# Silu and sigmoid of the second layer from exp and ln, in smaller steps, in a two-layer kernel on one core

## The chip, the cores and the metric

One core of one Trainium2 chip runs the kernel. The metric is the device time in microseconds: the median of three runs before is 5545.22 us (5544.22 to 5549.63).

## What is computed

The reference puts two layers on x (8 x 1024 x 256, float32). Layer 0 is a mixture of experts, causal attention and again the experts. Layer 1 is a channel mix, a selective scan and again the channel mix. The change touches layer 1 alone, of which this matters:

```python
# channel mix (before and behind the scan), on layernorm(x)
r = jax.nn.sigmoid(xr @ W_r.T)
out = r * (square(relu(xk @ W_k.T)) @ W_v.T)
# selective scan, 512 channels x 16 states
u, z = jnp.split(einsum('bld,ed->bel', h, in_proj_w), 2, axis=1)
uc = silu(causal_conv4(u) + conv_b)
delta = softplus(dt_proj(x_proj(uc)))
state = exp(delta * A) * state + delta * B * uc      # along 1024 steps
y = (sum_n state * C + uc * D) * silu(z)
```

## The kernel before

Layer 1 works by sequences (8), each in four chunks of 128 channels. 16 channels' worth of lines by 8 states lie on the 128 partitions, so that a chunk needs 16 scans along 1024 steps, a sequence 64 and the layer 512. `run` (L1597) writes the order of the scans out by hand. One turn of its loop is: `decay(i + 1)`, an exp by ACT (L1648) from a line spread by DMA into one of two PSUM tiles h; `feed(i + 2)`, a product by POOL (L1639); the scan by DVE (L1740), in place in h; the product hc with C by DVE (L1745), after which h is free. Every fourth turn PE adds the products up (L1665). Engines take their instructions in order, so this order is also the order of waiting.

All other work of the layer hangs in between as lists of steps, one Python generator each: "2before" is the channel mix of the next sequence, its normalisation, input projection and convolution (`steps_before`, with `steps_mix`); "1gate" is softplus of the next chunk and silu(z) of this one (`steps_gate`, `steps_delta`); "2low" the small projections; "3behind" what comes behind the scans. `Steps.turn` (L1578), called twice a turn, lets each list go on by its pace: a list collects due time at work / scans (L1717: 175 us in 48 scans for "2before"), each step takes its own estimate off, and at most three steps of a list go at once. What isn't through by its end is drained, all steps in a row (L1725, L1730). A step says what it needs: `hold` keeps PE and the two spare PSUM banks for its list until the next step, `gap` asks for turns of distance, `when` for a condition. For the first sequence nothing of this lies beside scans; its steps are drained before the first one (L1698, L1700).

`Pipe` (L1163) holds back the instruction that takes a full bank over until the next bank is filled. The three steps of this change go another way: both halves of a gate (L1286), of the convolution (L1391) and of z (L1442) are filled into both banks, and then one step of 3.8 us takes both over with the sigmoid (L1296) or silu (L1400, L1509), and calls `tables()` (L1154), which asks ACT for the table that holds exp and ln together:

```python
self.net.nc.scalar.preload_act_table_set("natural_log_exp_and_others")
```

`run` calls it once at its head too. Softplus (L1470 to L1484) is made of exp, ln and three POOL products in four pieces of 256 columns; its tile sp_e has one buffer.

Of the kernel before, what the change touches and what calls it, by code (L numbers as in the profile page):

```python
# [8 lines left out]
F32 = mybir.dt.float32  # L9
# [8 lines left out]
P = 128  # L18
# [20 lines left out]
DI = 512  # L39
# [1022 lines left out]
class Layer1:  # L1062
# [17 lines left out]
    def __init__(self, net, pool, Wr_t, Wk_t, Wv_t, mu_r, mu_k, ln_gamma, ln_beta, in_t, conv_w,  # L1080
                 conv_b, xp_t, dtp_t, dtp_b, A_log, Dp, out_t):
        self.net, nc = net, net.nc

        def column(name, ap, n):
            t = pool.tile([P, n], F32, name=name)
            nc.sync.dma_start(t, ap.rearrange("(c p) -> p c", p=P))
            return t

        self.mixed = {}
        for n, w, mu in (("r", Wr_t, mu_r), ("k", Wk_t, mu_k)):
            m = column(f"cm_m{n}", mu, KC)
            w0 = pool.tile([P, KC, D], F32, name=f"cm_w{n}0")
            nc.sync.dma_start(w0, w.rearrange("(k p) d -> p k d", p=P))
            w1 = pool.tile([P, KC, D], F32, name=f"cm_w{n}1")
            n1 = pool.tile([P, KC], F32, name=f"cm_n{n}")
            nc.vector.tensor_scalar(n1, m, -1.0, 1.0, ALU.mult, ALU.add)
            for k in range(KC):
                nc.vector.tensor_scalar(w1[:, k, :], w0[:, k, :], n1[:, k : k + 1], None, ALU.mult)  # L1100
                nc.vector.tensor_scalar(w0[:, k, :], w0[:, k, :], m[:, k : k + 1], None, ALU.mult)
            self.mixed[n] = (w1, w0)
        self.wv = pool.tile([P, KC, D], F32, name="cm_wv")
        nc.sync.dma_start(self.wv, Wv_t.rearrange("(k p) d -> p k d", p=P))
        self.gamma = column("ln_g", ln_gamma, KC)
        self.beta = column("ln_b", ln_beta, KC)
        self.conv_b = column("conv_b", conv_b, NDC)
        self.skip = column("skip", Dp, NDC)
        self.w_in = pool.tile([P, KC, 2 * DI], F32, name="w_in")
        nc.sync.dma_start(self.w_in, in_t.rearrange("(k p) e -> p k e", p=P))  # L1110
        self.taps = pool.tile([P, NDC, TAPS], F32, name="taps")
        nc.sync.dma_start(self.taps, conv_w.rearrange("(c p) o k -> p c (o k)", p=P))
        self.w_x = pool.tile([P, NDC, RK + 2 * NS], F32, name="w_x")
        nc.sync.dma_start(self.w_x, xp_t.rearrange("(c p) e -> p c e", p=P))


        self.XR = RK + 2 * NS
        self.w_dt = pool.tile([self.XR + 1, DI], F32, name="w_dt")
        nc.gpsimd.memset(self.w_dt[RK : self.XR, :], 0.0)
        nc.sync.dma_start(self.w_dt[0:RK, :], dtp_t)  # L1120
        nc.sync.dma_start(self.w_dt[self.XR : self.XR + 1, :], dtp_b.unsqueeze(0))
        self.w_out = pool.tile([P, NDC, D], F32, name="w_out")
        nc.sync.dma_start(self.w_out, out_t.rearrange("(c p) e -> p c e", p=P))

        n = DI // self.G
        self.A = pool.tile([P, self.PARTS, n], F32, name="A")
        with net.tc.tile_pool(name="l1_al", bufs=1) as once, net.tc.tile_pool(
            name="l1_a", bufs=1, space=PSUM
        ) as ps:
            al = once.tile([n, self.PARTS, P], F32, name="al")  # L1130
            a0 = once.tile([n, self.G, NS], F32, name="al0")
            nc.sync.dma_start(a0, A_log.rearrange("(i d) n -> i d n", d=self.G))
            pa = ps.tile([P, self.PARTS, n], F32, name="pa")
            for i in range(self.PARTS):
                nc.vector.tensor_copy(
                    al[:, i, :].rearrange("i (d n) -> i d n", n=self.NP),
                    a0[:, :, i * self.NP : (i + 1) * self.NP],
                )
                nc.tensor.transpose(pa[:, i, :], al[:, i, :], net.ident[0:n, 0:n])
            nc.scalar.activation(self.A, pa, AF.Exp)  # L1140
        nc.vector.tensor_scalar(self.A, self.A, -1.0, None, ALU.mult)

        one = pool.tile([P, self.G], F32, name="pick1")
        nc.vector.tensor_reduce(
            one, net.ident.rearrange("p (d n) -> p d n", n=self.NP), AX.X, ALU.add
        )
        self.pick = pool.tile([P, self.RG // self.G, self.RG], F32, name="pick")
        nc.gpsimd.memset(self.pick, 0.0)
        for j in range(self.RG // self.G):
            nc.gpsimd.tensor_copy(self.pick[:, j, j * self.G : (j + 1) * self.G], one)  # L1150
        self.minus = pool.tile([P, 1], F32, name="minus")
        nc.gpsimd.memset(self.minus, -1.0)
# [26 lines left out]
    def rsqrt(self, small, r, v):  # L1179
# [9 lines left out]
        nc.gpsimd.tensor_scalar(t, t, -0.5, 1.5, ALU.mult, ALU.add)  # L1189
        nc.gpsimd.tensor_tensor(r, r, t, ALU.mult)  # L1190

    def minus_mean(self, small, mv, r, name):

        off = small.tile([P, self.net.NT], F32, name=name)
        self.net.nc.gpsimd.tensor_tensor(off, mv[:, :, 0], r, ALU.mult)
        self.net.nc.gpsimd.tensor_scalar(off, off, -1.0, None, ALU.mult)
        return off
# [37 lines left out]
    def steps_mix(self, q, pools, pipe, x):  # L1235
# [20 lines left out]
        for t0 in range(0, T, W):  # L1256
# [21 lines left out]
            for i in range(0, W, 2 * P):  # L1278
# [10 lines left out]
                            )  # L1289
                got.append((i, pr))  # L1290
                pipe.filled(None)
            yield need(act=3.8, banks=True)
            gates = []
            for i, pr in got:
                r = pools["r"].tile([P, 2, D], F32, name="cm_r")
                nc.scalar.activation(r, pr, AF.Sigmoid)  # L1296
                gates.append((i, r))
            self.tables()
            for i, r in gates:
                yield need(pe=1.7, dve=0.7, pool=1.3)  # L1300
                pv = self.bank(pools, [P, 2, D], "pv")
# [15 lines left out]
    def steps_before(self, q, pools, pipe, load, keep_x):  # L1317
# [44 lines left out]
        for c in range(NDC):  # L1362
# [18 lines left out]
            tap = pools["tap"].tile([P, TAPS, P], F32, name="tap")  # L1381
            for k in range(TAPS):
                nc.scalar.mul(tap[:, k, :], net.ident, self.taps[:, c, k : k + 1])
            got = []
            for t0 in range(0, T, W):
                for k in range(TAPS):
                    if k % 2 == 0:
                        yield need(pe=1.7, hold=True, when=q.room)
                    if k == 0:
                        pc = self.bank(pools, [P, W], "pc")  # L1390
                    nc.tensor.matmul(  # L1391
                        pc, tap[:, k, :], u[:, k + t0 : k + t0 + W],
                        start=(k == 0), stop=(k == TAPS - 1),
                    )
                got.append((t0, pc))
                pipe.filled(None)
            yield need(act=3.8, banks=True, gap=1)
            o = pools["uc"].tile([P, T], F32, name="uc")
            for t0, pc in got:
                nc.scalar.activation(  # L1400
                    o[:, t0 : t0 + W], pc, AF.Silu, bias=self.conv_b[:, c : c + 1]
                )
            self.tables()
            q.uc.append(o)

    def steps_low(self, q, pools, pipe):
# [41 lines left out]
    def steps_delta(self, q, c, pools, pipe):  # L1448
# [22 lines left out]
        w = W // 2  # L1471
        for t0 in range(0, T, w):
            t = slice(t0, t0 + w)
            yield need(act=1.2, gap=1 if t0 else 0)
            e1 = pools["sp1"].tile([P, 2, w], F32, name="sp_e1")
            nc.scalar.activation(e1[:, 0, :], e[:, t], AF.Identity, bias=net.ones[:, 0:1])
            nc.scalar.activation(e1[:, 1, :], e1[:, 0, :], AF.Identity, bias=self.minus)
# [2 lines left out]
            nc.gpsimd.tensor_tensor(e1[:, 1, :], e1[:, 1, :], e[:, t], ALU.subtract)  # L1480
            nc.gpsimd.tensor_tensor(dl[:, t], dl[:, t], e1[:, 0, :], ALU.add)
            nc.gpsimd.tensor_tensor(dl[:, t], dl[:, t], e1[:, 1, :], ALU.subtract)
        yield need(pool=2.3, gap=1)
        nc.gpsimd.tensor_tensor(du, dl, q.uc[c], ALU.mult)  # L1484
        q.steps[c] = self.sent(pools, "dl", c, dl)
# [9 lines left out]
    def steps_gate(self, q, c, pools, pipe):  # L1495

        nc = self.net.nc
        T, W = self.net.T, self.W
        if c + 1 < NDC:
            yield from self.steps_delta(q, c + 1, pools, pipe)  # L1500
        got = []
        for t0 in range(0, T, W):
            yield need(pe=1.7, hold=True)
            got.append((t0, self.in_proj(q, pools, DI + c * P, t0)))
            pipe.filled(None)
        yield need(act=3.8, banks=True)
        q.zs = pools["zs"].tile([P, T], F32, name="zs")
        for t0, pz in got:
            nc.scalar.activation(q.zs[:, t0 : t0 + W], pz, AF.Silu)  # L1509
        self.tables()  # L1510

    def steps_behind(self, q, pools, pipe, load, store, when):

# [83 lines left out]
    def run(self, pools, load, load_x, keep_x, store):  # L1597
# [111 lines left out]
        for i, (b, c, l, p) in enumerate(order):  # L1709
            k = i % NS  # L1710
            if k == 2:
                if c == 0:
                    if b > 0:
                        side.drain("3behind")
                        side.add("3behind", behind(b - 1), 85, 56)
                    if b + 1 < B:
                        side.add("2before", before(b + 1), 175, 48)  # L1717
            if k == (0 if 0 < c < NDC - 1 else 2):
                side.add(
                    "1gate", self.steps_gate(seqs[b], c, pools, pipe),  # L1720
# [39 lines left out]
def kernel(  # L1760
# [102 lines left out]
    with ExitStack() as st:  # L1863
# [5 lines left out]
        with tc.manual_schedule():  # L1869
            with ExitStack() as ro:  # L1870
# [4 lines left out]
            name: pool_in(st, f"l1_{name}", bufs) for name, bufs in (  # L1875
                ("x", 2), ("mixT", 1), ("ka", 2), ("r", 2), ("hT", 2), ("u", 1), ("uc", 2 * NDC),
                ("xd", 1), ("delta", 1), ("du", 1), ("sp1", 1), ("zs", 1),
                ("rep", 1), ("sdl", 3), ("sdu", 3), ("dbu", 2), ("hc", 6), ("tap", 1), ("xn", 2), ("small", 2),
            )
        }  # L1880
        pools["dram"] = dram2
# [57 lines left out]
```

## Time and profile before

| what | us |
|---|---|
| median of three runs | 5545.22 |
| the profiled execution, its own time | 5545.59 |
| its span | 5543.9 |
| first scan starts (L1740) | 2920.8 |
| last product hc ends (L1745) | 5465.4 |
| ACT's table loads in lines of layer 1 | 194 x 1.283 |

The page gives the busy time of each engine (PE is the matrix engine, DVE, ACT and POOL the vector, activation and general engines). A row of a group has the line, the engine, the operation, the tiles as out<-in, the count, the busy time, the mean of one in ns, and behind the second bar the idle time of the engine ahead of it and who ended it. A row of the waits has who waited for whom, the sum in us, how often, and the longest. A row of the timeline has start and duration in us. In the row of a stage each engine has its busy time and count, followed by the granted clock of the matrix engine, the DMA share and GB/s.

### The profile page before, as it was taken

How to read it: one execution, taken by the hardware profiler on the slowest of the kernel's cores; microseconds unless marked ns; L12 is line 12 of the kernel's file. 1: busy time of each engine (PE TensorE's matmuls, PEld its weight loads, DVE VectorE, ACT ScalarE, POOL GpSimd, SP SyncE). 2: the span in 40 equal slices, each digit the busy share in tenths (PEclk: the TensorE clock that was granted, in tenths of full speed). 3: DMA queues.
4: the chain of work that ended last, by engine and by line, in shares of the span. 5: the costliest groups of instructions: out<-in, count | busy, mean ns of one | idle time of the engine just before them, and what ended most of it. 6: DMA issues, size and time to landing. Idle time of an engine off the chain costs nothing.

```text
span 5543.9 us, 60312 instructions
## 1 busy us (share of the span) xinstructions
PE 4501.1 (81%) x21046; PEld 2165.4 (39%) x21046; DVE 3400.8 (61%) x5590; ACT 2562.0 (46%) x4374; POOL 2388.7 (43%) x2089
## 2 busy tenths in 40 slices
PE   5699699999999998499766768788787778877767
PEld 5365434444444443265432233233333324333224
DVE  5632166666666764633107777778777777777884
ACT  2111145665566554011145646565564655646453
POOL 1244211111111111234317767667666766667773
PEclk6799889999999998699887889889898888989878
DMA  6133212212221221132205454535446464454652
GB/s 213 28 59 63 76 42 75 72 60 70 83 72 62 69 75 57 48 58 57 42 28 148 130 151 126 153 103 153 133 115 160 113 165 111 121 149 129 164 138 63
DMA packets 253570, 545.28 MB, mean 98 GB/s; under 512 B 30257, under 2 KB 144001, under 8 KB 253266
## 3 DMA queue, kind: packets, MB, share of 16 engines
q1 hardware_dynamic: 228690, 507.34, 33.1%
q0 software_dynamic: 24576, 34.10, 3.8%
q8 instruction: 166, 2.72, 0.2%
q14 instruction: 138, 1.13, 0.1%
HBM read 400.31 MB, written 141.03 MB: 98 GB/s over the span
## 4 chain that ended last, share of the span: by engine, by line
PE 23%; DVE 9%; ACT 7%; POOL 6%; issue 5%; DMA 3%; SPq 0%; DVEq 0%; POOLq 0%; ACTq 0%
DVE h L1740 6%; PE y L1665 4%; PE pc L1391 4%; PE pk L1264 3%; PE pr L1286 3%; PE pu L1442 2%; ACT h L1648 2%; DMA sdu<-du 1%; PE pp L1524 1%; POOL dbu L1639 1%; PE po L489 1%; DVE hc L1745 1%; PE px L1421 1%; ACT xn L1220 1%; PE pm L472 1%
## 5 line engine op out<-in xcount | busy, mean ns | idle before, releaser
L777 ACT ACTIVATE pT<-s 128x512 f32<-128x512 f32 (+3 forms) x1536 | 669.5, 489 | 522.9 <-PE s L734 513.7
L1665 PE MATMUL y<-hc,pick 128*32 128x512 f32 x2048 | 675.0, 739 | 280.4 <-DVE hc L1745 269.1
L734 PE MATMUL s<-kT,qT 32*128 32x512 f32 (+3 forms) x3072 | 829.9, 538 | 14.1 <-DVE mx L750 11.4
L1648 ACT ACTIVATE h<-sdl,A 128x1024 f32<-128x1024 f32 x512 | 567.6, 1113 | 510.8 <-DVE hc L1745 490.6
L1740 DVE TENSOR_TENSOR_SCAN h<-h,dbu 128x1024 f32<-128x1024 f32 x256 | 586.5, 2291 | 283.1 <-ACT h L1648 161.5
L734 PE MATMUL s<-qT,kT 32*128 32x512 f32 (+3 forms) x3072 | 743.4, 539 | 8.1 <-ACT pT L777 8.1
L1639 POOL TENSOR_TENSOR dbu<-sdu,b 128x1024 f32<-128x1024 f32 x256 | 602.5, 2354 | 284.6 <-DVE h L1740 142.0
L1740 DVE TENSOR_TENSOR_SCAN h<-h,sdu 128x1024 f32<-128x1024 f32 x256 | 586.4, 2290 | 186.6 <-ACT h L1648 149.0
L1745 DVE TENSOR_TENSOR hc<-h,c 128x1024 f32<-128x1024 f32 x512 | 626.0, 1223 | 48.1 <-DMA c<-bc 9.7
L783 POOL TENSOR_SCALAR_AFFINE_SELECT pT<-pT 128x512 f32<-128x512 f32 x256 | 162.4, 634 | 1136.5 <-ACT pT L777 1052.8
L1639 POOL TENSOR_TENSOR sdu<-sdu,b 128x1024 f32<-128x1024 f32 x256 | 602.4, 2353 | 14.8 <-DMA b<-bc 2.8
L734 PEld LDWEIGHTS s<-kT,qT 32*128 32x128 f32 x3072 | 319.6, 186 | 434.9 <-DVE mx L750 188.6
L476 ACT ACTIVATE mid<-pm,bu 128x512 f32<-128x512 f32 x192 | 131.6, 686 | 728.8 <-PE pm L472 721.3
L747 DVE TENSOR_REDUCE part<-s 128x1 f32<-128x512 f32 x512 | 329.2, 685 | 178.5 <-PE s L734 177.9
L1665 PEld LDWEIGHTS y<-hc,pick 128*32 128x32 f32 x2048 | 133.5, 127 | 774.8 <-DVE hc L1745 386.7
L497 POOL DMA_INDIRECT acc<-o,idx x128 | 210.5, 1644 | 495.5 <-DVE o L494 240.6
L750 DVE CUSTOM_DVE_ANT_0 junk<-s,mask,part 128x256 f32<-128x256 f32 (+3 forms) x512 | 281.5, 550 | 157.5 <-PE s L734 112.6
L472 PE MATMUL pm<-tT,wu 128*128 128x512 f32 x768 | 362.4, 609 | 0.0
L489 PE MATMUL po<-wd,mid 128*128 128x256 f32 x1536 | 350.4, 392 | 0.0
L750 DVE CUSTOM_DVE_ANT_0 junk<-s,mask 128x256 f32<-128x256 f32 (+3 forms) x512 | 250.5, 489 | 138.9 <-PE s L734 86.7
L797 PE MATMUL po<-pT,at_v 128*32 128x512 f32 (+3 forms) x3072 | 329.5, 501 | 0.7 <-POOL pT L783 0.4
L1442 PE MATMUL pu<-hT,w_in 128*128 128x512 f32 x512 | 269.1, 667 | 63.7 <-DVE cm_r L1310 48.7
(261 smaller groups left out, 6778.8 us busy)
## 6 DMA issues: line engine op xcount, KB each, us to landing
sdl<-dl SPq DMA_DIRECT2D x256, 512.0 KB
sdu<-du SPq DMA_DIRECT2D x256, 512.0 KB
acc<-xt SPq DMA_DIRECT2D x24, 1024.0 KB
xt<-acc SPq DMA_DIRECT2D x24, 1024.0 KB
rows<-moe_r SPq DMA_DIRECT2D x16, 1056.0 KB
qT<-padded_q SPq DMA_DIRECT2D x32, 512.0 KB
kT<-padded_k SPq DMA_DIRECT2D x32, 512.0 KB
kept<-so SPq DMA_DIRECT2D x64, 256.0 KB
```

The lines of the kernel that those rows point to most:

```text
L472: nc.tensor.matmul(pm, wu[:, k, n * P : (n + 1) * P], tT[:, k, t0 : t0 + HALF], start=(k == 0), stop=(k == KC - 1),)
L489: nc.tensor.matmul(po, mid[:, n, j * P : (j + 1) * P], wd[:, n, :], start=(n == 0), stop=(n == NF - 1),)
L734: self.net.nc.tensor.matmul(s[:, 0 : rhs.shape[-1]], lhsT, rhs, start=True, stop=True)
L750: nc.vector.tensor_tensor_reduce(junk[:, 0:w], sh[:, 0:w], self.mask[:, W - w : W], 1.0, part if a else -3e38, ALU.add, ALU.max, self.mx[n ...
L777: self.net.nc.scalar.activation(pT[:, h, 0:w], sh[:, 0:w], AF.Exp, scale=1.0 / HD**0.5)
L797: nc.tensor.matmul(q.po[h * HS : (h + 1) * HS, o:W], self.va[q.b % 2][:, j, g * HG + h, :], pT[:, h, 0 : W - o], start=(j == 0), stop=(j = ...
L1442: self.net.nc.tensor.matmul(pu, self.w_in[:, k, e0 : e0 + P], q.hT[:, k, t0 : t0 + self.W], start=(k == 0), stop=(k == KC - 1),)
L1639: nc.gpsimd.tensor_tensor(inputs[i], t, seqs[b].rep["b", p], ALU.mult)
L1648: nc.scalar.activation(decays[i], spread["dl", i - p], AF.Exp, scale=self.A[:, p, n : n + 1])
L1665: nc.tensor.matmul(self.py[g * self.RG : (g + 1) * self.RG, t0 : t0 + W], self.pick[:, j, :], hc[:, t0 : t0 + W], start=(j == 0 and p == 0 ...
L1740: nc.vector.tensor_tensor_scan(decays[i], decays[i], inputs.pop(i), 0.0, ALU.mult, ALU.add)
L1745: nc.vector.tensor_tensor(hc, decays.pop(i), seqs[b].rep["c", p], ALU.mult)
```

## The change

Sigmoid and Silu as table functions go, with the three calls of `tables()` behind them; the call at the head of `run` stays. 1 / (1 + exp(-x)) is computed as exp(-ln(1 + exp(-x))), three ACTIVATEs. For a gate these stand in three small steps, exp and ln for each of two tiles and then both last exps. For uc and z the bank is taken over through `Pipe` by Identity with bias or a copy, and a new function `silu` works on the result in SBUF: in four pieces of 256 columns for uc (factor tile in a pool "sg" of its own), in two of 512 for z (factor tile in the pool of softplus). POOL multiplies. A list `busy` marks a pool whose one tile is in use, and steps of softplus and silu wait for it. The pace of "2before" goes from 175 to 215 us.

```diff
+    def silu(self, x, pool):
+        nc = self.net.nc
+        w = x.shape[-1]
+        yield need(act=0.2 + 0.002 * w, when=lambda: pool not in self.busy)
+        self.busy.append(pool)
+        s = pool.tile([P, w], F32, name="sigmoid", tag="sp_e1")
+        nc.scalar.activation(s, x, AF.Exp, scale=-1.0)
+        nc.scalar.activation(s, s, AF.Ln, bias=self.net.ones[:, 0:1])
+        yield need(act=0.1 + 0.001 * w, pool=0.1 + 0.0024 * w, gap=1)
+        nc.scalar.activation(s, s, AF.Exp, scale=-1.0)
+        nc.gpsimd.tensor_tensor(x, x, s, ALU.mult)
+        self.busy.remove(pool)
...
-            yield need(act=3.8, banks=True)
             gates = []
             for i, pr in got:
+                yield need(act=1.2, banks=True)
                 r = pools["r"].tile([P, 2, D], F32, name="cm_r")
-                nc.scalar.activation(r, pr, AF.Sigmoid)
+                nc.scalar.activation(r, pr, AF.Exp, scale=-1.0)
+                nc.scalar.activation(r, r, AF.Ln, bias=net.ones[:, 0:1])
                 gates.append((i, r))
-            self.tables()
+            yield need(act=1.2)
+            for i, r in gates:
+                nc.scalar.activation(r, r, AF.Exp, scale=-1.0)
...
-                got.append((t0, pc))
-                pipe.filled(None)
-            yield need(act=3.8, banks=True, gap=1)
-            o = pools["uc"].tile([P, T], F32, name="uc")
-            for t0, pc in got:
-                nc.scalar.activation(
-                    o[:, t0 : t0 + W], pc, AF.Silu, bias=self.conv_b[:, c : c + 1]
-                )
-            self.tables()
+                pipe.filled(lambda t0=t0, pc=pc: nc.scalar.activation(
+                    o[:, t0 : t0 + W], pc, AF.Identity, bias=self.conv_b[:, c : c + 1]
+                ))
+            yield need(act=0.6, banks=True, gap=1)
+            pipe.flush()
+            w = W // 2
+            for t0 in range(0, T, w):
+                yield from self.silu(o[:, t0 : t0 + w], pools["sg"])
...
-            yield need(act=1.2, gap=1 if t0 else 0)
+            yield need(act=1.2, gap=1 if t0 else 0, when=lambda: pools["sp1"] not in self.busy)
+            self.busy.append(pools["sp1"])
...
+            self.busy.remove(pools["sp1"])
...
-        yield need(act=3.8, banks=True)
-        q.zs = pools["zs"].tile([P, T], F32, name="zs")
-        for t0, pz in got:
-            nc.scalar.activation(q.zs[:, t0 : t0 + W], pz, AF.Silu)
-        self.tables()
+            pz = self.in_proj(q, pools, DI + c * P, t0)
+            pipe.filled(lambda t0=t0, pz=pz: nc.scalar.copy(q.zs[:, t0 : t0 + W], pz))
+        yield need(act=0.6, banks=True)
+        pipe.flush()
+        for t0 in range(0, T, W):
+            yield from self.silu(q.zs[:, t0 : t0 + W], pools["sp1"])
...
-                        side.add("2before", before(b + 1), 175, 48)
+                        side.add("2before", before(b + 1), 215, 48)
```

More of the change, by code (lines that the diff above doesn't have):

```diff
@@ L1082, in __init__ @@
         self.net, nc = net, net.nc
+        self.busy = []
         def column(name, ap, n):
@@ L1383, in steps_before @@
                 nc.scalar.mul(tap[:, k, :], net.ident, self.taps[:, c, k : k + 1])
-            got = []
+            o = None
             for t0 in range(0, T, W):
@@ L1387, in steps_before @@
                     if k % 2 == 0:
-                        yield need(pe=1.7, hold=True, when=q.room)
+                        yield need(pe=1.7, act=0.3, hold=k == 0, when=q.room)
+                    if o is None:
+                        o = pools["uc"].tile([P, T], F32, name="uc")
                     if k == 0:
@@ L1500, in steps_gate @@
             yield from self.steps_delta(q, c + 1, pools, pipe)
-        got = []
+        q.zs = None
         for t0 in range(0, T, W):
-            yield need(pe=1.7, hold=True)
-            got.append((t0, self.in_proj(q, pools, DI + c * P, t0)))
-            pipe.filled(None)
-        yield need(act=3.8, banks=True)
-        q.zs = pools["zs"].tile([P, T], F32, name="zs")
-        for t0, pz in got:
-            nc.scalar.activation(q.zs[:, t0 : t0 + W], pz, AF.Silu)
-        self.tables()
+            yield need(pe=1.7, act=0.6)
+            if q.zs is None:
+                q.zs = pools["zs"].tile([P, T], F32, name="zs")
+            pz = self.in_proj(q, pools, DI + c * P, t0)
[4 more added lines that the diff above has]
+            yield from self.silu(q.zs[:, t0 : t0 + W], pools["sp1"])
     def steps_behind(self, q, pools, pipe, load, store, when):
@@ L1877 @@
                 ("xd", 1), ("delta", 1), ("du", 1), ("sp1", 1), ("zs", 1),
-                ("rep", 1), ("sdl", 3), ("sdu", 3), ("dbu", 2), ("hc", 6), ("tap", 1), ("xn", 2), ("small", 2),
+                ("rep", 1), ("sdl", 3), ("sdu", 3), ("dbu", 2), ("hc", 6), ("tap", 1), ("sg", 1), ("xn", 2), ("small", 2),
             )
```

## Prediction

> **What bounds the kernel now.** I read the page first, then the busy times of the second attention layer's scans, the waits of DVE there, ACT's timeline through one gate, and the groups of ACT's table loads.
>
> ```profile
> span 5543.9 us, 60312 instructions
> PE 4501.1 (81%) x21046; PEld 2165.4 (39%) x21046; DVE 3400.8 (61%) x5590; ACT 2562.0 (46%) x4374; POOL 2388.7 (43%) x2089
> ```
>
> The change touches only what lies behind 2759 us. Its core is the stage from the first scan (2920.8) to the last product (5465.4), 512 scans. Busy times there, in the order PE, PEld, DVE, ACT, POOL:
>
> ```profile
> 2921.00:5465.00 2544.00, 1928.80 (x5774) 827.55 (x5774) 1927.70 (x1474) 1435.67 (x2019) 1751.40 (x1329) 0.86 0.52 135
> ```
>
> No engine is full: DVE and PE 76%, POOL 69%, ACT 56%. A scan and its product take DVE 2.29 + 1.22 us, about 3.5 us a turn, but a turn lasts 2544/512 = 4.97 us. DVE's waits in this stage tell why:
>
> ```profile
> DVE h L1740 <- ACT h L1648: 310.4, 127, 5.5
> DVE xt L1528 <- PE pp L1524: 119.3, 18, 14.1
> DVE uc L1676 <- PE y L1665: 78.3, 22, 7.2
> DVE h L1740 <- POOL delta L1481: 26.0, 7, 3.7
> ```
>
> The largest is for the decay that ACT makes for each scan. Two decays fit into PSUM, so ACT can be one scan ahead, no more; whatever ACT does between two decays beyond some 2.4 us delays the scan. One gate shows it:
>
> ```profile
> 3263.43 1.12 ACT L1648 ACTIVATE h<-sdl,A 128x1024 f32<-128x1024 f32 x1 [3.17 <-DVE hc L1745]
> 3264.49 0.58 ACT L1272 ACTIVATE ka<-pk 128x512 f32<-128x512 f32 x1
> 3265.10 0.63 ACT L1273 ACTIVATE ka<-ka 128x512 f32<-128x512 f32 x1
> 3265.74 1.28 ACT L1509 ACT_TABLE_LOAD   x1
> 3268.96 0.60 ACT L1509 ACTIVATE zs<-pu 128x512 f32<-128x512 f32 x1 [1.93 <-PE pu L1442]
> 3274.43 0.60 ACT L1509 ACTIVATE zs<-pu 128x512 f32<-128x512 f32 x1 [4.88 <-PE pu L1442]
> 3275.05 1.28 ACT L1156 ACT_TABLE_LOAD   x1
> 3276.34 1.12 ACT L1648 ACTIVATE h<-sdl,A 128x1024 f32<-128x1024 f32 x1
> ```
>
> Two loads and two waits for PE put 12.9 us between two decays. That is what the change means to remove. Whether it does depends on the loads, so I looked at who causes them:
>
> ```profile
> L1156 ACT ACT_TABLE_LOAD x96 | 123.2, 1283 | 1.7
> L619 ACT ACT_TABLE_LOAD x16 | 20.5, 1283 | 0.3
> L620 ACT ACT_TABLE_LOAD x16 | 20.5, 1283 | 0.3
> L1183 ACT ACT_TABLE_LOAD x1 | 1.3, 1283 | 0.0
> ```
>
> L1156 is tables(), which asks for the table that has exp and ln together; it is called 97 times and has 96 loads. The call missing is the one at the head of run: behind it the first ln (L1183) and the first exp (L1184) loaded a table each, and only after the first gate's call do ln and exp run without loads. L619 and L620 are an ln and an exp in the first attention, under a call of the same kind (L964) made once at its head: both load, 16 times of 16. So in this program a call at the head doesn't last; a pair of ln and exp costs two loads unless a call stands right before it.
>
> **What the change really does to the tables.** It removes the 96 calls inside the stage and keeps the one at the head. The built order of instructions of both programs (a list by engine, loads included, no times) settles what follows. For the kernel before it lists 237 loads, line by line those of the trace. For the changed one it lists 827: every ln of silu (192), every ln of a gate (64), 201 of the 512 decays, 111 of the ln of softplus, and so on. Layer 1 has 784 where it had 194, +590; of these before the first scan 48 (were 14), between the first and last decay 726 (were 176), behind them 10 (were 4).
>
> **ACT in the scan stage.** A load: 1.28, and 1.29 from start to start in the timeline.
> Loads: (726 - 176) x 1.29 = +710 us.
> Silu of uc, 112 pieces of 256: an ACTIVATE on 256 columns takes 0.42 without a bias (L1478) and 0.51 with one (L1477); exp, ln with its bias, exp: 0.42 + 0.51 + 0.42 = 1.35, +151. The 56 passes over PSUM stay (Identity with bias for Silu).
>
> ```profile
> L1477 ACT ACTIVATE sp_e<-sp_e,minus 128x256 f32<-128x256 f32 x128 | 65.0, 508 | 4.2
> L1478 ACT ACTIVATE sp_e<-sp_e 128x256 f32<-128x256 f32 x128 | 53.3, 417 | 4.1
> L1273 ACT ACTIVATE ka<-ka 128x512 f32<-128x512 f32 x64 | 40.3, 630 | 2.0
> ```
>
> Silu of zs, 64 pieces of 512: at the step from start to start of such rows (0.50, with a bias 0.59) 1.59, +102; a copy stands for the old Silu. Gates: one ln and one exp more for 56 tiles, 1.09, +61.
> Sum: 1436 + 710 + 151 + 102 + 61 = 2460 us. That alone is 97% of the stage as it is, on an engine that is 44% idle only because it waits for others.
>
> How much of it DVE feels: I summed ACT's steps between each two decays and DVE's between each two scans, in the built order, with these durations, and took the larger of each pair. Before: 2218; the stage took 2545, so 327 us are waits that this sum doesn't hold (PE above all). After: 3011. In 252 turns of 512 ACT is the longer, by 1004 us together (before 143 turns, 211 us); in 142 turns it holds over 7 us (before 7). An ACTIVATE ahead of a load also loses the 0.1 us by which its like overlap (0.58 takes 0.48 from start to start): 726 more of these give 3082.
>
> Of the 327 us I keep half, 163. For less: a PE that ACT holds back has its result ready sooner, and uc and zs now leave PSUM one fill later, so the waits for pc (70.3) and pu (74.8) shrink. For more: each silu piece reuses one factor tile, and its first exp waits until POOL has made the product before; softplus does the same and waits 116.5/128 = 0.9 us a piece, 160 us for 176 pieces. Behind that exp the next decay is queued, and DVE waits for it. Stage: 3082 + 163 = 3245, +700.
>
> **POOL, PE, DMA.** POOL gains 112 x 0.73 (L1480) + 64 x 1.27 (L1311) = 163 us: 1914 of 3245, no bound. A product that waits for ACT's exp has the inputs of the next scans queued behind it, but those are made two scans ahead, 7 us; cost nothing here, and at most that of the 26.0 us row doubled where the cover is gone. PE's matmuls stay, their holds get shorter; no DMA is added or moved past another. The pace of 215 instead of 175 only keeps the longer list of steps on time. The flag keeps silu and softplus from each other's tile: between nothing and the 0.9 us a piece counted above; I take nothing more.
>
> **Prologue and end.** Before the first scan nothing hides ACT: DVE idles 108.5 us there. A chunk of 128 channels takes 11.6 us there (from one L1383 at 2832.1 to the next at 2843.7). Each of its four pieces takes 0.45 + 1.29 + 0.54 + 1.29 + 0.45 + 0.9 for the product = 4.9, the last 4.0: 18.7, less the load that goes (1.3) and a wait for PE (1.4): +16, four times: +64. Two gates +4 each, four loads of the normalisations +5, one for softplus +1: +78. The end behind the last scan: two gates +9, two loads +3: +12. Together +90.
>
> 5543.9 + 700 + 90 = 6334; the profiled execution's own time is 1.7 us above its span, and the median of the runs 5545.2 lies there too: 6335.
>
> **Two rules against the rows.** The Trainium skill (ScalarE: Activation LUTs, Table sets: the hidden batching unit) counts one load for ln and exp, as one set has both. By it the stage has no loads: the sum of the longer ones falls to 2179, and the kernel gets faster. The rows L619 and L620 show two loads for such a pair, so I go by them. The same page (What ACT_TABLE_LOAD costs) has about 2.66 us a switch with a drain; the timeline has the next ACTIVATE 1.29 us after a load's start. By the rule the sum would be 3986 and the time over 7200.
>
> **Rivals.**
> Faster: one table serves all on the chip, loads listed or not. 2179 - 2218 = -39, at 2545/2218 -45; half of the waits for pc and pu goes, -73; prologue without loads about +26: 5450. For it stand the 96 calls after which ln and exp don't load; against it the built order, which matched before line by line. It decides by the count: from 0 loads (5450) to 726 (6335) is 1.2 us a load, so below some 80 loads in the stage. 4%.
> Absorbed: ACT's 1108 idle us take the 1024 added, only prologue and end stay: 5635. Against it: those pauses wait for hc (490.6 us), and one decay ahead is all the slack there is. 2%.
> Smoother: ACT and DVE even out over two turns (the sum is then 2901) and no other wait is on top: 5544 + 356 + 90 = 5990. 20%.
> Nothing of the other waits goes: 3082 + 327, up to 3082 x 1.147 = 3536: 6500 to 6625. 22%.
> By the page's 2.66 us: over 7200. 2%.
> My forecast, 6335 (6180 to 6460): 50%. The range reaches from 6040 to 6570. A measurement can tell 0.2% from no change: faster 0.04, same 0.01, slower 0.95.
>
> **What would show it.** After: some 784 loads of 1283 ns from layer 1's lines, none from tables(); ACT over 70% busy in a scan stage of about 3245 us, DVE about 60%; DVE's wait for ACT's decay up from 310 to some 1000 us or more; the first scan about 80 us later. I am wrong if the loads aren't there, or if ACT still idles a third of the stage while the time is near 6000.

## Result, and the profile after

The changed kernel takes 6593.5 us (median of four runs, 6589.9 to 6597.1), before 5547.4: ratio 1.188, 95% interval 1.187 to 1.190. The forecast was 6335, range to 6570; the rise is 1046 us instead of 790.

Page, the row of the scan stage (first scan 3002.9, last product about 6507), and DVE's waits in that stage:

```profile
span 6595.4 us, 61811 instructions
PE 4651.1 (71%) x21046; PEld 2201.5 (33%) x21046; DVE 3408.6 (52%) x5590; ACT 3688.3 (56%) x5668; POOL 2558.0 (39%) x2281
```

```profile
3003.00:6507.00 3504.00, 2059.64 (x5776) 859.97 (x5778) 1936.97 (x1475) 2480.42 (x3210) 1912.61 (x1505) 0.75 0.38 98
```

```profile
DVE h L1762 <- ACT h L1670: 1102.7, 212, 14.1
...
DVE xt L1550 <- PE pp L1546: 160.1, 18, 17.7
DVE cm_r L1328 <- ACT cm_r L1316: 129.3, 7, 20.4
DVE uc L1698 <- PE y L1687: 56.0, 15, 5.4
```

ACT has the 2480 us that were forecast (2460), and they fill 71% of a stage that is 960 us longer. DVE's own time is within 10 us of that before; its wait for the decay grew from 310 to 1103 us, and seven waits for the gates' last exp are new. The first scan comes 82 us later (forecast 78), and the part behind the stage is 10 us longer (forecast 12).

The two largest groups of loads, and ACT between two decays:

```profile
L1670 ACT ACT_TABLE_LOAD x201 | 257.9, 1283 | 3.6
L1201 ACT ACT_TABLE_LOAD x192 | 246.3, 1283 | 3.4
```

```profile
3666.75 1.05 ACT L1489 ACTIVATE du<-du 128x1024 f32<-128x1024 f32 x1
3667.82 0.51 ACT L1496 ACTIVATE sp_e<-du,ones 128x256 f32<-128x256 f32 x1
3668.37 0.51 ACT L1497 ACTIVATE sp_e<-sp_e,minus 128x256 f32<-128x256 f32 x1
3668.89 1.28 ACT L1498 ACT_TABLE_LOAD   x1
3670.19 0.42 ACT L1498 ACTIVATE sp_e<-sp_e 128x256 f32<-128x256 f32 x1
3670.62 1.28 ACT L1311 ACT_TABLE_LOAD   x1
3671.91 0.60 ACT L1311 ACTIVATE cm_r<-pr 128x512 f32<-128x512 f32 x1
3672.53 1.28 ACT L1312 ACT_TABLE_LOAD   x1
3673.82 0.72 ACT L1312 ACTIVATE cm_r<-cm_r,ones 128x512 f32<-128x512 f32 x1
3674.56 1.28 ACT L1670 ACT_TABLE_LOAD   x1
3675.86 1.12 ACT L1670 ACTIVATE h<-sdl,A 128x1024 f32<-128x1024 f32 x1
```

Four loads lie in 8 us, ahead of a decay that DVE needs. So the loads are there, each as long as before. Whether they are all of it, the experiments had to say.

### The profile page after: what moved, and what is told of

It reads as the page before. It is cut to its first block, busy times and chain, and to the rows that moved or that the text cites. A ratio compares the mean times of both kernels' runs of the same rounds, so it can differ in the third digit from the quotient of the medians.

```text
span 6595.4 us, 61811 instructions
## 1 busy us (share of the span) xinstructions
PE 4651.1 (71%) x21046; PEld 2201.5 (33%) x21046; DVE 3408.6 (52%) x5590; ACT 3688.3 (56%) x5668; POOL 2558.0 (39%) x2281
## 4 chain that ended last, share of the span: by engine, by line
ACT 22%; PE 17%; issue 7%; POOL 7%; DVE 5%; DMA 3%; SPq 0%; POOLq 0%; DVEq 0%; ACTq 0%
PE pc L1411 4%; DVE h L1762 3%; ACT h L1670 3%; PE pu L1461 3%; ACT L1670 3%; ACT L1201 3%; PE pk L1279 2%; PE y L1687 2%; PE pp L1546 2%; DMA sdu<-du 2%; ACT sigmoid L1201 1%; PE pr L1301 1%; ACT sigmoid L1200 1%; POOL dbu L1661 1%; POOL uc L1204 1%
## 5 line engine op out<-in xcount | busy, mean ns | idle before, releaser
L1687 PE MATMUL y<-hc,pick 128*32 128x512 f32 x2048 | 688.6, 754 | 487.3 <-DVE hc L1767 477.7
L1461 PE MATMUL pu<-hT,w_in 128*128 128x512 f32 x512 | 315.5, 752 | 270.7 <-ACT u L1393 106.2
L1411 PE MATMUL pc<-u,tap 128*128 128x512 f32 x512 | 271.9, 682 | 253.3 <-ACT tap L1401 238.4
L1243 PE MATMUL tr<-ident,xn 128*128 128x128 f32 x384 | 112.1, 406 | 375.0 <-ACT xn L1235 348.2
```

The source lines that it names most:

```text
L1411: nc.tensor.matmul(pc, tap[:, k, :], u[:, k + t0 : k + t0 + W], start=(k == 0), stop=(k == TAPS - 1),)
L1461: self.net.nc.tensor.matmul(pu, self.w_in[:, k, e0 : e0 + P], q.hT[:, k, t0 : t0 + self.W], start=(k == 0), stop=(k == KC - 1),)
L1687: nc.tensor.matmul(self.py[g * self.RG : (g + 1) * self.RG, t0 : t0 + W], self.pick[:, j, :], hc[:, t0 : t0 + W], start=(j == 0 and p == 0 ...
```

## Experiments

The names "pin" mean kernels with the loads taken out. Times are medians; "before" ran beside them at 5548 to 5555 us.

### The loads out, some put back, and some put into the kernel before

pin_all, in `rsqrt`, once in the program:

```diff
+        self.set = False
...
         nc.scalar.activation(r, v, AF.Ln)
+        if not self.set:
+            self.set = True
+            self.tables()
```

> The changed kernel with one call of tables() more, right behind the first ln of layer 1 (in rsqrt): the built order then has 2 table loads in layer 1 instead of 784, every other instruction the same. If the loads are the cause: below the kernel before, 5450 to 5520 (the sum of the longer of ACT and DVE per turn is 2179 against 2218 before; the ratio 1.139 of the stage to the sum, which held before and after, makes 2482 of it, the prologue adds some 26). If the finer steps, the waits for POOL's products or PE's lower clock cost by themselves: above 5800, and the load-free kernel keeps a good part of the 1046 us.

5894.6 us, ratio 1.062 (1.060 to 1.064). The loads are worth 6593.5 - 5894.6 = 699 us, 0.89 us for each of the 782 that are gone. But what I expected of a kernel without them falls, and the rival stands: it isn't faster than the kernel before, it is 343 us slower. Its scan stage takes 2859 us with a sum of 2179, a ratio of 1.31 (the sum is the prediction's: the longer of ACT's and DVE's steps, turn by turn); that 1.139 fitted both the kernel before and the changed one was chance.

pin_dose, in `silu`:

```diff
+        nc.scalar.preload_act_table_set("exp_and_others")
         nc.scalar.activation(s, s, AF.Exp, scale=-1.0)
+        self.tables()
```

> The kernel of pin_all with loads put back by hand: in silu the last exp is made in the table of exp alone and the table of both is asked for behind it; 386 loads in layer 1, 352 of them in the scan stage, all else the same. If a load costs in proportion: sum 2625 x 1.139 = 2990 for the stage, prologue +65, together about 6060, 1.5 us a load over pin_all. If loads were mostly hidden and the steps cost: within 100 us of pin_all.

6247.7 us: +353 us for 384 loads, 0.92 us each, less than the 1.5 expected. With all else alike, half of the loads cost half as much.

before_no_calls, at all three places:

```diff
-            self.tables()
```

> The kernel before without its three calls of tables() behind the gates; its steps stay coarse, and loads come before exp and ln wherever another table is active: 474 in layer 1 (194 with the calls), 460 in the scan stage (176). If loads are the cause wherever they stand: sum 2543 x 1.139 = 2897 for the stage, about 5895. If it is the fine steps: about 5545, as no step changes.

5765.5 us, ratio 1.039 (1.037 to 1.041): +214 us for 280 loads, 0.77 each. The kernel with the coarse steps pays for loads too, less than expected. The ratio of stage to sum is 1.08 here (2746 to 2543) and 1.21 in pin_dose (3186 to 2625), so it is no constant.

### What else costs: the parts given back

The profile of pin_all, DVE's waits and ACT's in the scan stage:

```profile
DVE h L1766 <- ACT h L1674: 524.9, 168, 10.0
...
DVE cm_r L1332 <- ACT cm_r L1320: 66.9, 7, 10.9
```

```profile
ACT uc L1419 <- PE pc L1415: 161.8, 50, 5.1
ACT sp_e L1500 <- POOL delta L1506: 153.4, 39, 8.9
ACT sigmoid L1204 <- POOL uc L1208: 99.7, 84, 4.4
```

ACT's timeline shows softplus and the silu of z taking turns in their one tile:

```profile
3613.63 0.42 ACT L1502 ACTIVATE sp_e<-sp_e 128x256 f32<-128x256 f32 x1
3615.93 0.63 ACT L1204 ACTIVATE sigmoid<-zs 128x512 f32<-128x512 f32 x1 [1.88 <-POOL delta L1506]
3616.59 0.72 ACT L1205 ACTIVATE sigmoid<-sigmoid,ones 128x512 f32<-128x512 f32 x1
3617.22 1.10 ACT L1674 ACTIVATE h<-sdl,A 128x1024 f32<-128x1024 f32 x1
3618.26 0.61 ACT L1207 ACTIVATE sigmoid<-sigmoid 128x512 f32<-128x512 f32 x1
3620.25 0.51 ACT L1500 ACTIVATE sp_e<-du,ones 128x256 f32<-128x256 f32 x1 [1.37 <-POOL zs L1208]
```

No load here, but 1.9 us of waiting for POOL ahead of one decay and 1.4 us ahead of the next: each time ACT writes the tile again only when POOL has read it.

pin_uc_back, pin_zs_back and pin_gate_back each put one of the three parts back to the code of before (removed lines of the diff above return), so each adds 64 loads:

> The kernel of pin_all with the silu of uc alone made as before (both banks held, Silu of ACT, tables() behind it: 64 loads). pin_all stands 344 us above the kernel before with hardly a load, so something else costs. Theory, round trips: a silu of pieces through one factor tile makes ACT wait for POOL's product and POOL for ACT, with decays queued behind; of ACT's added waits in pin_all's stage 100 us are for the product of uc and 91 us for pc. Then this gives most of it back: 5680 to 5750. Rival, work: what counts is ACT's own time (151 us less here, 72 us of loads more): 5790 to 5830.

> The kernel of pin_all with the silu of z alone made as before (Silu and tables(): 64 loads). Its factor shares the tile of softplus, the two lists take turns in it, and ACT waits for POOL at every change of hands (19 + 27 + 15 us in rows of their own, and 153 against 111 for softplus itself). Theory, round trips: 5740 to 5810. Rival, work: ACT has 102 us less and 83 us of loads more: 5860 to 5895.

> The kernel of pin_all with the gates alone made as before (Sigmoid and tables(): 64 loads). No POOL product is in it, so by the theory of round trips this part gives nothing back and the loads cost: 5895 to 5960. By the rival that the smaller steps of every kind cost: below 5850.

5771.1, 5775.3 and 5859.1 us: they give back 123, 119 and 36 us, in spite of the added loads. The two silus are the most of it. uc gave less and z as much as the round trips said, and the gate gave some where they said none.

pin_both_back, both silus as before:

> The kernel of pin_all with both silus as before, so that only the gates are made of exp and ln in small steps, with the pace of 215. If the parts add up: 5895 - 123 - 119 = 5653. If the two silus hinder each other (softplus and silu of z share a tile, both wait for POOL), less is given back by the second: 5700 or more; if each alone had still kept the other's loads dear: below 5620.

5700.2 us: the second gives back 71 to 75 instead of about 120. The parts don't add up, and even with the gates alone changed 150 us remain, those of the pace of 215 included.

pin_gap:

```diff
-        yield need(act=0.2 + 0.002 * w, when=lambda: pool not in self.busy)
+        yield need(act=0.2 + 0.002 * w, gap=1, when=lambda: pool not in self.busy)
```

> The kernel of pin_all, but every silu piece starts at the earliest one turn behind the product of the piece before (gap=1 at the first step of silu), so that POOL has made it. Theory, round trips: ACT's waits for the products of uc and z (114 us) go, about 5790; the list takes more turns, and if more of it is drained in a row at its end, it gives that back. Rival: no change, within 40 us of 5895.

5813.8 us, -81. A turn of distance hides part of the round trip: ACT's wait for POOL's product of uc falls from 99.7 to 54.3 us.

pin_no_product leaves out POOL's multiplication in silu, so that uc and silu(z) are not what the reference has:

```diff
-        nc.gpsimd.tensor_tensor(x, x, s, ALU.mult)
```

> The kernel of pin_all without POOL's product in silu; it leaves out the multiplication x * sigmoid(x), so that uc and silu(z) are wrong, and ACT's three passes and all steps stay. In the turns of pin_all in which DVE waits for a decay, ACT idles 241 us for POOL (43 in the kernel before) and as long for PE as before (249 against 268). Theory, round trips through POOL: most of that goes, 5680 to 5780. Rival, ACT's own work and the list's pace: within 50 us of 5895.

5714.8 us, -180. ACT's three passes are all there, so the product of POOL, and the waiting on it, is worth these 180. Which of the two it is, POOL's own time or the wait, this run can't tell.

conv_late, the changed kernel with the convolution's banks held and taken over as before:

```diff
-                        yield need(pe=1.7, act=0.3, hold=k == 0, when=q.room)
+                        yield need(pe=1.7, hold=True, when=q.room)
...
-                pipe.filled(lambda t0=t0, pc=pc: nc.scalar.activation(
-                    o[:, t0 : t0 + W], pc, AF.Identity, bias=self.conv_b[:, c : c + 1]
-                ))
+                got.append((t0, pc))
+                pipe.filled(None)
...
```

> The changed kernel, loads as in it, but the convolution's two banks are held until both are full and taken over in one step, as before. ACT waited 154 us for pc in the changed kernel's stage (70 before). If that wait is what the forecast left out: 80 to 150 us below 6593. If the waits beyond the sum grow in proportion to it, whichever they are: the sum is 3104 instead of 3082, and the time stays within 60 us of 6593.

6610.0 us, 16 more. Where ACT takes pc over, and how long the banks are held, is not what was missed. The wait for pc itself was hardly touched (142 us instead of 155), so what that wait costs stays untested.

### The pace

before_pace, the kernel before with one number changed:

```diff
-                        side.add("2before", before(b + 1), 175, 48)
+                        side.add("2before", before(b + 1), 215, 48)
```

> The kernel before with the pace of the list of the next sequence at 215 instead of 175 and nothing else. The three parts given back one by one returned 123, 119 and 36 us of the 344, so up to 70 are left for what they share: the pace. If it counts: 5600 to 5640 (more of the list crowds into the turns that ACT already limits; the sum of the longer ones rises from 2234 to 2296). If not: 5530 to 5560.

5670.4 us, ratio 1.022 (1.021 to 1.024): +120 us for a number that removes no work and adds none. DVE's wait for the decay in its stage:

```profile
DVE h L1740 <- ACT h L1648: 487.3, 127, 10.5
...
DVE uc L1676 <- PE y L1665: 12.8, 7, 2.0
```

As many waits as before (127), but 487 us instead of 310; the wait for y is 66 us shorter, and all of DVE's waits together are some 117 us longer, which is the loss. By the trace, the last uc of the next sequence is taken over at scan 40 of 64 instead of scan 49; the same steps crowd into fewer turns. That the crowding is the cause is not shown: a slower pace costs as much in gates_coarse165 below.

Of the 150 us left in pin_both_back, 120 are thus the pace's; 30 remain for the gates' small steps, although 64 loads are gone there.

The same number back to 175 in three other kernels:

> The kernel of pin_all with the pace of 175 instead of 215. If the pace costs here what it costs the kernel before: 5895 - 120 = 5775. If the longer list needs the faster pace and is otherwise drained in a row before the last chunk's end: 5895 or more.

> The kernel of pin_all at the pace of 175 and without POOL's product in silu (the multiplication x * sigmoid(x) is left out, uc and silu(z) are wrong). If pace and round trips together are the whole of the 344: 5895 - 120 - 180 = 5595 or below, near the kernel before. If they are the same thing measured twice: 5700.

> The changed kernel, loads as in it, with the pace of 175. If the pace is a part of the 1046 us: about 6475. If ACT, filled by loads, sets the time at either pace: within 40 us of 6593.

5798.6 (-96), 5658.0 and 6491.9 us (-102, with 14 loads more). The pace is worth as much with the loads as without. Without product and at 175, the kernel is still 110 us over the one before; pace and round trips aren't the whole.

The pace doesn't act through the same wait everywhere. In the changed kernel DVE's wait for the decay is no shorter at 175 (1117 us, at 215 1103); there its wait for the gates' last exp falls from 129 to 35 us, and in pin_all from 67 to 10, the wait for the decay from 525 to 498. A wait shows where time is lost; how much, only the sum of DVE's waits tells.

### A version that gains

gates_coarse, the kernel before with its gates from exp and ln in one step, without their 32 calls, and a lasting call as in pin_all:

> The kernel before with the gates alone made of exp and ln, in the one step of 3.8 us as before, without their call of tables(); a lasting call behind the first ln. 64 loads go (83 us of ACT), two ACTIVATEs for each of 64 tiles come (70 us); sum of the longer ones 2217 against 2234. No product of POOL is in it. If that is all: 5500 to 5545. If exp and ln in the gate cost by the longer step between two decays: above 5560.

5548.2 us, ratio 0.9998 (0.9987 to 1.0010): no change that can be measured. Its pace at 165 and at 185:

> The kernel of gates_coarse at a pace of 165 instead of 175. If slower is better down to where the list is drained: 5515 to 5535. If 175 is already the least: 5550 to 5600 (the sum of the longer ones rises from 2217 to 2267).

> The kernel of gates_coarse (5548) at a pace of 185. If the time rises evenly from 175 to 215 (120 us in 40): 5575 to 5585. If the lowest lies between: below 5545. If the times jump with the pace, as other steps fall together: above 5600.

5643.5 and 5555.7 us, ratios 1.017 (1.015 to 1.019) and 1.0002 (0.9990 to 1.0013). Between 175 and 185 the time doesn't change, but 165 costs 95 us and 215, in the kernel before, 120. At 185 the wait for the decay is 392 us instead of 301 all the same, made up for by DVE's other waits (that for y: 5 instead of 76); at 165 it is 458. At 165 the last uc comes at scan 51, at 185 at scan 46. Why 165 costs so much is open.

gates_attn is gates_coarse with a lasting call behind the first ln of the first attention too:

> The kernel of gates_coarse with a lasting call of the table of ln and exp behind the first ln of the first attention as well: 2 loads there instead of 32, nothing else. If every load costs some 1.2 us, as in the changed kernel's scan stage: 5510 to 5515. If only a load that a late ACT has before a decay costs: within 8 us of 5548.

5544.9 us, ratio to before 0.9978 (0.9968 to 0.9988). It is the only version below the kernel before, by some 12 us. That is 0.4 us for each of 30 loads, between what the two expected, and half of the 0.89 that a load cost in the changed kernel. The gain is that of the first attention, not of the gates: the scan stage has the same 2548 us as in gates_coarse, and from the attention's first ln to its last takeover (so) the trace has 1502 us, in the nineteen other kernels 1514 to 1520. That is some 15 us, or 0.5 a load.

## Why the forecast was wrong

**Right: that the loads are there, and what they do to ACT.** There are 784 loads in layer 1, 1283 ns each, as the built order listed, and the direction with them. ACT's busy time in the stage came out within 20 us, the prologue and the end within 4 and 2. The sum of the longer ones holds as well: 3082 forecast, 3085 with the durations of the trace.

**Mis-sized: "Of the 327 us I keep half, 163."** The stage took 3504 us, so 422 lie beyond the sum of 3082. The 259 that are missing are the whole error. They divide in two: with the pace at 175 the stage takes 3406 us on a sum of 3099 (from the trace), so some 307 lie beyond it, and the halving alone cost the forecast 144; the pace of 215 brings the other 115. The waits for PE that were to shrink did not: that for pc grew and that for pu stayed (75 before, 70 after).

```profile
ACT uc L1400 <- PE pc L1391: 70.3, 36, 2.8
```

```profile
ACT uc L1415 <- PE pc L1411: 154.5, 50, 6.0
```

The wait for POOL was named (0.9 us a piece, 160 us) but set off against them. I added up, over the turns in which a scan waits for its decay, what ACT did since the decay before (worked out from the timeline and its releasers):

| kernel | DVE waits | ACT busy | ACT waits for PE | ACT waits for POOL |
|---|---|---|---|---|
| before | 310 | 489 | 268 | 43 |
| before_pace | 487 | 597 | 319 | 112 |
| pin_all | 525 | 585 | 249 | 241 |
| pin_pace175 | 498 | 567 | 312 | 176 |
| pin_no_product | 401 | 523 | 248 | 110 |
| pin_noprod175 | 369 | 470 | 293 | 50 |
| changed | 1103 | 1362 | 244 | 171 |

The wait for PE stays near 250 to 320 whatever was done. The wait for POOL rises most from before to pin_all, by 198 us; ACT's busy time rises by 96. Without the product the wait for POOL falls by some 130 at either pace, with the pace of 175 by some 60; without both it is back at 50. Leaving the product out gives 180 us at the pace of 215 and 141 at 175. What the product costs in the changed kernel, beside the loads, was not measured.

**Wrong: "The pace of 215 instead of 175 only keeps the longer list of steps on time."** I costed this edit at nothing. It is worth 120 us in the kernel before, 96 without loads, 102 in the changed one, which at 175 takes 6492, inside the range. The edit has no instruction of its own, so a sum of durations can't hold it. Nor does the sum by turns: from the durations of the traces it rises by 59 for the kernel before (2262 to 2321), and for the changed one it points the other way (3099 at 175, 3085 at 215).

**The rivals.** 6593 lies in the range of "Nothing of the other waits goes" (6500 to 6625), whose upper end is the sum times the ratio of the stage to it before. Its premise fits the waits for PE, and the 307 at the pace of 175 beside the 327; but the pace is not in it, and the ratio is 1.31 without loads. That it met the number is luck in good part. "Faster: one table serves all" (5450) stands for the kernel without loads, from which the price of a load was taken. That kernel takes 5895: I let the load-free sum (2179 against 2218) stand for the time, and round trips and pace are not in it. It was taken 445 us too fast, and the loads 186 too dear (885 instead of 699, or 1.2 us each instead of 0.89), which leaves the same 259. The loads add 903 us to the sum (2179 to 3082) but 645 to the stage (2859 to 3504): 680 us lie beyond the sum in pin_all and 422 in the changed kernel. So loads do fill time that would else have been waiting, but from 680 us down, not from 327.

**Slips in the working.** The sum of 3082 has 0.1 us of lost overlap for each load, that of 2218 has not; with it the sum before is 2234, and 311 us lie beyond it, not 327. Of the 96 calls, 88 are inside the stage. And a pair of ln and exp does not need a call right before it: in the kernel before, L1183 and L1184 load once each in 32 pairs, and in pin_all one call behind the first ln lasts for the layer. Why a call at the head does not, no run shows.

So the 1046 us, one after the other: 110 from the kernel before to pin_noprod175, 141 for POOL's product, 96 for the pace, 699 for 782 loads. The order matters: product first and pace second, they are 180 and 57 the other way round. In the 110 are 192 loads fewer than in the kernel before, which at 0.77 us would be 148 to the good; so longer chains on ACT, smaller steps and takeovers by the pipe cost some 260, by this estimate, 14 of it ahead of the first scan (174 us from the first ln of layer 1, before 160). What each of these, and the lower clock of the matrix engine (below), has of it was not separated, nor why the gate alone, in pin_gate_back, was worth 36; the 30 us in pin_both_back point the same way.

## What to carry to other kernels

Count table loads in the built order of instructions, not in the source: here a call for the shared table at the head did not last, and one behind the first ln took out 782 loads. Before replacing a function of ACT by a chain with a product on another engine, look at what waits for ACT in its order: a factor tile with one buffer can turn a piece into a round trip ahead of the next decay. A pace that only deals out work is an edit like any other; try it alone, on the kernel before.

## What was not expected of the hardware

The same load of 1283 ns costs the kernel 0.89 us in the changed kernel, 0.92 in pin_dose, 0.77 in the kernel before without its calls and 0.4 to 0.5 in the first attention. The granted clock of the matrix engine in the scan stage was 0.86 before, 0.81 in pin_all and 0.75 in the changed kernel, while PE was busy 76%, 69% and 59% of it. A matmul of the convolution took 606, 696 and 675 ns there, so it does not simply follow the clock. How much of the time the clock explains was not tried.
